# A two-layer vision tower on one core: the tokenizer's second chunk on 64 rows, layer 1's folded value weights earlier, the last image's rows ahead of its gate, and the last output rows on two queues

## The chip, the core and the metric

The kernel runs on one core of a Trainium2 chip. Five engines work side by side, each through its own instructions in order: PE (TensorE, matmuls and transposes; its weight loads are listed apart as PEld), DVE (VectorE), ACT (ScalarE), POOL (GpSimd) and SP (SyncE, which here only issues transfers). ACT, POOL and SP can each issue DMA transfers. The metric is the device time of one execution in microseconds (us). All data are 32-bit floats.

## What is computed

The input is four images of 3 x 224 x 224. Cut to what matters here, the reference does:

```python
patches = ...                               # [4, 784, 192], 8x8 pixels x 3 channels
t = layernorm(patches) @ W1 + b1            # 192 -> 256
t = layernorm(t)
t = concatenate([t, t, t], axis=1)          # 2352 tokens an image, three equal copies
h = silu(layernorm(t @ Wp1 + bp1)) @ Wp2 + bp2
# layer 0: softmax attention between the images (heads of 32), then an expert FFN
h = h + attn0(layernorm(h))                 # q, k, v, a sigmoid gate, output weights Wo
h = h + ffn0(layernorm(h))                  # router, top 2 of 6 experts, three matmuls each
# layer 1: linear attention, then a shared MLP and top 2 of 4 small experts
h = h + attn1(layernorm(h))                 # q, k, v from W_qkv; k^T v; (v + t2) @ W_out
h = h + ffn1(layernorm(h))
```

The three copies of a token are equal, so the kernel computes 4 x 784 tokens and writes each row three times.

## The kernel before

**Tiles.** An image's 784 tokens are six tiles of 128 and 16 rows left over. The leftover rows of all four images share a 25th tile, LT, in segments of 32 partitions. The rows h live in SBUF from the tokenizer to the end.

**Start.** The images arrive by DMA in `img` with 126 partitions (patch rows of the images, with gaps). `flatten` (L381) copies them into `vT`, group by group (7 groups of 4 patch columns), on DVE (groups 0, 3, 5) or ACT (1, 2, 4, 6); a patch takes 193 columns there: 192 pixels and, as the last, its standard deviation, which `patch_stats` (L487, DVE) and `patch_stds` (L494 to L497 on DVE, a square root L498 on ACT) make. `turn_patches` transposes a group on PE (L393) and copies it on ACT (L397) into `pT`: chunk 0 has 128 rows (pixels), chunk 1 has 65 (64 pixels and the deviation). `first_layers`, a generator that the stage advances with `next(steps)`, meanwhile folds the first layer norm into the weights `Wall`, 512 columns wide: 256 for the product and 256 that carry it on through Wp1.

**Tokenizer.** `first_steps` takes the tiles in seven groups `turns` of 4, 4, 4, 4, 3, 3 and 3. For each tile it runs two matmuls (L637), chunk 0 then chunk 1, then squares on ACT (L640); a square root (L642), DVE's `y` (L648 to L652), a second root (L655) and `xn` (L659) follow, then `turned_rows` (silu) and `last_rows`.

**Zero-fill.** The expert stage scatters rows into two DRAM buffers, `xrows` and `yrows`, which must be zero first. SP issues 46 transfers (L597) from an SBUF tile of zeros, `nothing`; each waits for `arrived[-1]`, the last patch statistics. Their SBUF bytes are later taken over by others: one of the buffers of `prod` (L907) lies on `nothing`.

**Layer 0's attention** begins while the tokenizer runs: `keys_values` makes keys (L320, pkv), values and gates of a group from its norm (L283 to L294, L701), adds the output bias to h (L1361), and `products` (L907, DVE) multiplies queries and keys of pairs of images. Then, image by image (s), come the shares of the softmax, `gate_act` (the gate's activation), `first_value`, `values`, `attended` (output weights, L989; sums of squares, L995), `rows_of_part` (the next norm's rows, L1025), `turn_part` (their transposes), the router, `choose`, `count` and `send` (POOL's scatters into xrows, L1154). For the last image the first expert blocks are woven in: `load` fetches a block's rows (L1498), `own_weights` (L1519) its weights, `hidden` (L1543, L1549) the hidden layers, `rows_back` (L1561, L1567) the last.

**Layer 1** takes units of three tiles and the leftover unit LU. `qk_mm` (L2001, PE), `qk_add` (L2007, DVE), `qk_squares` (L2015, L2016, ACT), `root` (L2033, ACT), `factors` (L2039 to L2043, DVE), `q_rows` (L2055, DVE) and `k_rows` (L2048, ACT) make normalised queries and keys; `stats_one` (L1767, L1784, L1785) sums a tile's expert outputs into h and takes its norm's statistics; `norm_root` is L1797 on ACT, and `norm_rows` L1806 and L1809 on DVE. `layer1_weights` is a generator of three steps: PE transposes the value weights (L812) and ACT copies them and a bias (L818, L819); PE multiplies them with the output weights (L825) and ACT copies the result Wvo (L829); the same for the bias (L834 to L837). Later, `k_x` (L2100), the norm of the keys (L2118 to L2126), Wvo and the output rows follow.

**FFN of layer 1** ends with the sums into h (L2410, L2415) and the output transfers (L2423). In the last group they alternate between SP's queue and ACT's; LT, the last tile, needs four transfers of 16 rows.

**What sets the order.** In these stages the order of each engine is that in which the program is written, by blocks `with tc.manual_schedule(engines=by_hand)` for DVE, PE and ACT (some for SP or POOL too). A moved call moves its instructions in every engine's queue at once.

Of the kernel before, what the change touches and what calls it, by code (L numbers as in the profile page):

```python
# [24 lines left out]
ALU = mybir.AluOpType  # L25
# [47 lines left out]
def tile_vit_tower(ctx: ExitStack, tc: tile.TileContext, a: dict, out: bass.AP):  # L73
# [296 lines left out]

    SROW = PD - P
    K1 = (P, SROW + 1)
    NPX = PD + 1
    flat = vT.rearrange("p c n -> p (c n)")[:IP, : HP * NPX].rearrange("q (w f) -> q w f", f=NPX)

    flattened = []

    def flatten(k, put):  # L380
        done = put(  # L381
            flat[:, k * PW : (k + 1) * PW, :PD].rearrange("q w (y x) -> q w y x", x=PATCH),
            img[:, :, k * PW * PATCH : (k + 1) * PW * PATCH].rearrange(
                "q y (w x) -> q w y x", x=PATCH
            ),
        )
        if put != nc.scalar.copy:
            flattened.append(done.ins.name)

    def turn_patches(k, c, put=nc.scalar.copy):  # L390
        pt, n = ps_tile("ptp"), K1[c]
        for j in range(PW):
            nc.tensor.transpose(  # L393
                pt[:n, j * IP : (j + 1) * IP], flat[:, k * PW + j, c * P : c * P + n],
                ident[:IP, :IP],
            )
        put(  # L397
            pT[:n, c, :, k * PW : (k + 1) * PW].rearrange("p (o h) w -> p o h w", o=SETS),
            pt[:n, : PW * IP].rearrange("p (w h o) -> p o h w", w=PW, h=HH)[:, :SETS],
        )  # L400

    def first_layers():

# [67 lines left out]
        for i in range(2):  # L471
# [2 lines left out]
            )  # L474
        nc.vector.memset(Wall[:, 0, D - 1 : D], 0.0)
        nc.vector.tensor_scalar(
            Wall[:, 1, D - 1 : D], ident[:, SROW : SROW + 1], math.sqrt(1e-5 * D), None, ALU.mult
        )
        yield
        nc.vector.tensor_tensor(bp1, pw, bp1, ALU.add)  # L480
# [9 lines left out]
    def patch_stds(k0, k1):  # L490
        w0, n = k0 * PW, (k1 - k0) * PW
        st, v = pst[:, w0 : w0 + n], pv[:, w0 : w0 + n]
        d = tokp.tile([IP, HP], F32, tag="pd", name="pd", bufs=2)[:, :n]
        nc.vector.tensor_tensor(d, st[:, :, 1], st[:, :, 4], ALU.subtract)  # L494
        nc.vector.tensor_tensor(v, st[:, :, 2], st[:, :, 5], ALU.add)
        nc.vector.scalar_tensor_tensor(d, d, PD / 4.0, d, ALU.mult, ALU.mult)
        nc.vector.tensor_tensor(v, v, d, ALU.add)  # L497
        nc.scalar.activation(  # L498
            flat[:, w0 : w0 + n, PD], v, AF.Sqrt, bias=eps[:IP], scale=1.0 / PD,
        )  # L500

    srow = tokp.tile([1, P], F32, tag="srow", name="srow")
# [5 lines left out]
    by_hand = {ENG.DVE, ENG.PE, ENG.Activation}  # L508
    with tc.manual_schedule(engines=by_hand):
        nc.vector.memset(srow, 0.0)  # L510
        nc.vector.memset(srow[:, SROW : SROW + 1], 1.0)
        nc.vector.memset(perm, 0.0)
        nc.vector.memset(perm[:, :, :PD], -1.0 / PD)
        by_y = ident[:KP, :KP].rearrange("p (y x c) -> p c y x", x=PATCH, c=CH)
        for half in range(2):
            nc.vector.tensor_scalar(
                perm[:, half, :PD].rearrange("p (c y x) -> p c y x", c=CH, x=PATCH)[
                    :, :, 4 * half : 4 * (half + 1)
                ],
                by_y, -1.0 / PD, None, ALU.add,  # L520
            )
        nc.scalar.activation(root_, one_, AF.Sqrt, bias=one_)
# [10 lines left out]
        flatten(0, nc.vector.tensor_copy)  # L533
        flatten(1, nc.scalar.copy)
        turn_patches(0, 0)
        for k in range(2):
            patch_stats(k)
        flatten(2, nc.scalar.copy)
        turn_patches(1, 0)
        for k in (3, 5):  # L540
            flatten(k, nc.vector.tensor_copy)
        next(steps)
        for k in range(2, cut0):
            patch_stats(k)
        turn_patches(2, 0)
        flatten(4, nc.scalar.copy)
        turn_patches(3, 0)
        flatten(6, nc.scalar.copy)
# [6 lines left out]
        for k in range(cut0):  # L555
            turn_patches(k, 1)
        for k in range(cut0, NK):
            patch_stats(k)
        next(steps)
        patch_stds(cut0, NK)  # L560
        for k in range(cut0, NK):
            turn_patches(k, 1)
# [51 lines left out]
    for c, n in enumerate(K1):  # L614
        nc.vector.tensor_copy(pL[:n, c, :, :LEFT], left(pTf[:n, c, :]))

    def pixels(c, t):
        if t == LT:
            return pL[: K1[c], c].rearrange("p b n -> p (b n)")
        n0 = t // TPI * SEQ + t % TPI * TT  # L620
        return pTf[: K1[c], c, n0 : n0 + TT]

# [4 lines left out]
    def first_steps(g):  # L627

        tiles = turns[g]
        n = len(tiles)  # L630
        y = tokp.tile([TT, GT, D], F32, tag="y", name="y", bufs=2)
        r = small.tile([TT, GT], F32, tag="rstd", name="rstd")[:, :n]
        pms = []
        for j in range(n):
            pm = ps_tile("pw1")[:TT]
            for c in range(2):
                nc.tensor.matmul(  # L637
                    pm, pixels(c, tiles[j]), Wall[: K1[c], c, :], start=(c == 0), stop=(c == 1)
                )
            nc.scalar.activation(sq1, pm[:, :D], AF.Square, accum_out=r[:, j : j + 1])  # L640
            pms.append(pm)
        nc.scalar.activation(r, r, AF.Sqrt, scale=1.0 / D, bias=zero[:TT])  # L642
        yield
        nc.vector.reciprocal(r, r)
        st = small.tile([TT, GT, 6], F32, tag="st", name="st")
        mv = small.tile([TT, GT, 2], F32, tag="mv", name="mv")
        for j in range(n):
            nc.vector.scalar_tensor_tensor(  # L648
                y[:, j, :], pms[j][:, D:], r[:, j : j + 1], bp1, ALU.mult, ALU.add
            )  # L650
            nc.vector.bn_stats(st[:, j, :], y[:, j, :])
# [929 lines left out]
    with tc.manual_schedule(engines=by_hand | {ENG.SP}):  # L1581
        gate_mm(s, 0)
        gate_mm(s, 1)
        products(s, 1, [1])
        expert_weights([2])
        scales_of(u)
        steps = early_blocks()
        next(steps)
        products(s, 1, [2])
        shifts_of(u)  # L1590
        next(steps)
        gate_act(s, 0)
        products(s, 1, [3])
        expert_weights(range(3, E0))
        next(steps)
        mx = shares_before(s)
        next(steps)
        gate_act(s, 1)
        shares_after(s, mx)
    att.close()  # L1600
    work[0] = layer0.enter_context(tc.tile_pool(name="blocks", bufs=2, reuse_waits="tile"))
# [4 lines left out]
    )  # L1606
    with tc.manual_schedule(engines=by_hand | {ENG.SP}):
        first_value(s, 0, 0, GN, nc.vector)
        first_value(s, 1, 0, GN, nc.scalar)
        rows_of_part(u)  # L1610
        values(s, 0, 0, GN)
        for _ in steps:
            pass
        for i in range(4):
            load(i)
        values(s, 1, 0, GN)
        turn_part(u)
        for o in range(2):
            first_value(s, o, *rest, nc.scalar)
        router(u)  # L1620
# [590 lines left out]
    with tc.manual_schedule(engines=by_hand | {ENG.Pool}):  # L2211
        x_t(1)
        for j in range(UT):
            qk_mm(0, j)
            qk_add(0, j)
            qk_squares(0, j)
        root(0)
        for j in range(UT):
            qk_mm(1, j)
        qk_add(1, 0)  # L2220
        qk_squares(1, 0)
        stats_one(LU, 0)
# [12 lines left out]
        root(1)  # L2235
        q_rows(0)
        stats_one(2, 0)
        next(steps)
        x_t(LU)
        q_t(0)  # L2240
        k_rows(0)
        next(steps)
        stats_one(2, 1)
        factors(1)
        q_rows(1)
# [113 lines left out]
    with tc.tile_pool(name="ffn1", bufs=2) as work:  # L2359
# [3 lines left out]
        for g, tiles in enumerate(parts):  # L2363
# [50 lines left out]
            for j, t in enumerate(tiles):  # L2414
# [4 lines left out]
                cuts = [(b, i * TT, 0, TT)]  # L2419
                if t == LT:  # L2420
                    cuts = [(k, TPI * TT, k * SEG, LEFT) for k in range(NI)]
                for k, s0, p0, rows_ in cuts:
                    eng.dma_start(  # L2423
                        out=out[k].rearrange("(k s) d -> s k d", k=REP)[s0 : s0 + rows_],
                        in_=h[p0 : p0 + rows_, t, :].unsqueeze(1).to_broadcast([rows_, REP, D]),
# [34 lines left out]
```

## Time and profile before

| what | us |
|---|---|
| median of 11 runs | 716.35 (715.01 to 719.26) |
| the profiled execution | 716.19 |
| its span | 714.5 |
| PE busy (matmuls) | 684.7, 96% of the span |
| PE weight loads | 474.5, 66% |
| DVE busy | 459.0, 64% |
| ACT busy | 331.4, 46% |
| POOL busy | 129.0, 18% |
| granted clock of PE, mean | 0.994 |

The profile comes from one execution, and its span runs from the first instruction to the end of the last; 1.69 us of the execution's time lie outside it. A row of a timeline has the start and the duration in us, the engine, the line of the program, the operation, what it writes and reads, its shape, how many instructions are joined in it, and in brackets the idle time ahead of it and what ended that. A group by line has, behind the bar, the busy time of the whole group in us, the mean of one in ns, and the idle time before. A row of the chain has start, duration and what was running, or what was waited for ("SPq" and "DVEq" are an engine's queue between a release and the start).

### The profile page before, as it was taken

The page shows a single profiled execution, that of the slowest core. Times are in us where ns is not written, and L with a number is a line of the kernel's source. Part 1 is how long each engine was busy: PE and PEld are TensorE (multiplying, and loading weights), DVE is VectorE, ACT ScalarE, POOL GpSimd, SP SyncE. Part 2 cuts the span into 40 slices and gives each one's busy share as a digit, 9 for nine tenths or more (in the row PEclk, how much of TensorE's full clock was granted, in tenths as well). Part 3 has the DMA queues.
Part 4 walks back from the last instruction along what each step waited for, and adds up shares of the span by engine and source line. Part 5 has one row for each costly group of instructions (what it writes and reads, how often), then busy time and mean ns, then how long its engine had stood idle before and what let it go on. Part 6 is the DMA issues. An engine that isn't in the chain of part 4 may idle for free.

```text
span 714.5 us, 9849 instructions
## 1 busy us (share of the span) xinstructions
PE 684.7 (96%) x3043; PEld 474.5 (66%) x3043; DVE 459.0 (64%) x1385; ACT 331.4 (46%) x816; POOL 129.0 (18%) x242
## 2 busy tenths in 40 slices
PE   7899999999999899999999998999999999999996
PEld 4646665566656678788888865667767844555553
DVE  5567785769888754457655658789869555344442
ACT  1556666556896664323222328464446132222321
POOL 5400000000045537300003218454000000000000
PEclk9999999999999899999999999999999999999999
DMA  5999999000034745322334342222000013332333
GB/s 185 286 426 424 425 424 424 27 1 0 0 100 158 265 156 180 122 83 97 96 106 143 102 132 81 68 66 67 0 1 1 4 31 122 121 100 72 112 99 91
DMA packets 56476, 96.49 MB, mean 135 GB/s; under 512 B 6696, under 2 KB 46350, under 8 KB 56424
## 3 DMA queue, kind: packets, MB, share of 16 engines
q1 hardware_dynamic: 49924, 79.69, 31.3%
q0 software_dynamic: 5600, 14.32, 6.6%
q10 hardware_dynamic: 900, 1.86, 0.8%
q8 instruction: 24, 0.39, 0.2%
q14 instruction: 28, 0.23, 0.1%
HBM read 30.75 MB, written 65.09 MB: 134 GB/s over the span
## 4 chain that ended last, share of the span: by engine, by line
PE 63%; DMA 16%; DVE 13%; ACT 4%; issue 2%; SPq 1%; ACTq 0%; DVEq 0%
DMA yrows<-nothing 14%; PE pb L1543 13%; PE pe L320 6%; PE pyb L1561 6%; PE ps L320 5%; PE pqk L2001 4%; PE ps L2410 3%; PE pt L311 3%; PE pout L2180 3%; PE pout L2185 3%; DVE oT L960 3%; PE pukx L2100 2%; PE pkv L320 2%; DMA img<-in_x_dram 2%; PE pe L2380 2%; PE ps L2404 2%
## 5 line engine op out<-in xcount | busy, mean ns | idle before, releaser
L1154 POOL DMA_INDIRECT xrows<-xn,pos x50 | 55.0, 1101 | 207.4 <-DVE nm L1010 172.6
L1753 POOL DMA_INDIRECT ys<-yrows,pos x50 | 49.5, 991 | 129.6 <-DMA yrows<-yb 115.3
L1549 ACT ACTIVATE hb<-pb,own 128x256 f32<-128x256 f32 (+1 forms) x74 | 33.6, 456 | 50.4 <-PE pb L1543 38.5
L1543 PE MATMUL pb<-xTb,own 128*128 128x256 f32 (+1 forms) x240 | 52.7, 362 | 2.0 <-DVE own L1519 1.3
L1543 PE MATMUL pb<-hb,own 128*128 128x256 f32 (+1 forms) x240 | 53.0, 360 | 0.3 <-DVE hb L1551 0.2
L1561 PE MATMUL pyb<-own,hb 128*128 128x256 f32 x216 | 52.3, 381 | 0.3 <-ACT hb L1549 0.2
L1543 PEld LDWEIGHTS pb<-xTb,own 128*128 128x128 f32 x240 | 41.9, 190 | 7.4 <-ACT junk L995 1.7
L320 PE MATMUL pe<-xT,eW 128*128 128x512 f32 (+1 forms) x112 | 46.0, 553 | 0.0
L2001 PE MATMUL pqk<-Wqkv,lxT 128*128 128x512 f32 x100 | 44.9, 594 | 0.2 <-ACT lxT L94 0.2
L1561 PEld LDWEIGHTS pyb<-own,hb 128*128 128x128 f32 x216 | 40.1, 190 | 6.3 <-ACT hb L1549 1.1
L1543 PEld LDWEIGHTS pb<-hb,own 128*128 128x128 f32 x240 | 40.7, 190 | 4.7 <-DVE hb L1551 0.9
L1567 DVE TENSOR_TENSOR yb<-pyb,eb 128x512 f32<-128x512 f32 (+1 forms) x30 | 19.1, 637 | 37.1 <-PE pyb L1561 35.3
L637 PE MATMUL pw<-Wall,pT 128*128 128x512 f32 (+1 forms) x96 | 42.4, 592 | 0.0
L1532 ACT COPY xTb<-ptb 128x512 f32<-128x512 f32 (+1 forms) x30 | 16.2, 541 | 53.6 <-PE ptb L1528 53.6
L907 DVE SCALAR_TENSOR_TENSOR prod<-kq 128x784 f32<-128x784 f32 x32 | 30.6, 969 | 7.3 <-ACT kq L882 3.9
L320 PEld LDWEIGHTS pe<-xT,eW 128*128 128x128 f32 x112 | 20.2, 190 | 21.6 <-issue 16.5
L1519 DVE COPY own<-kq 128x1540 f32 x30 | 29.0, 969 | 6.7 <-ACT xTb L1532 3.2
L311 PEld LDWEIGHTS pt<-ident,xn 128*128 128x128 f32 x200 | 24.3, 145 | 12.6 <-issue 6.9
L1551 DVE TENSOR_SCALAR hb<-pb,own 128x256 f32<-128x256 f32 (+1 forms) x46 | 20.3, 444 | 17.9 <-PE pb L1543 17.3
L637 PEld LDWEIGHTS pw<-Wall,pT 128*128 128x128 f32 (+1 forms) x96 | 17.9, 189 | 20.5 <-issue 18.5
L2001 PEld LDWEIGHTS pqk<-Wqkv,lxT 128*128 128x128 f32 x100 | 18.4, 190 | 19.3 <-issue 17.0
L2015 ACT ACTIVATE qk<-qk 128x256 f32<-128x256 f32 x50 | 20.4, 408 | 22.9 <-DVE qk L2007 20.8
(420 smaller groups left out, 1447.7 us busy)
## 6 DMA issues: line engine op xcount, KB each, us to landing
xrows<-nothing SPq DMA_DIRECT2D x22, 896.0 KB
yrows<-nothing SPq DMA_DIRECT2D x22, 896.0 KB
out_dram<-h SPq DMA_DIRECT2D x23, 384.0 KB
xb<-xrows SPq DMA_DIRECT2D x24, 256.0 KB
yrows<-yb SPq DMA_DIRECT2D x24, 256.0 KB
kq<-in_L_ffn_expert_w_dram SPq DMA_DIRECT2D x18, 256.0 KB
wb<-wd SPq DMA_DIRECT2D x16, 128.0 KB
img<-in_x_dram SPq DMA_DIRECT2D x5, 294.0 KB
```

Of the source, the lines that this page charges most:

```text
L311: nc.tensor.transpose(pt[:, j * TT : (j + 1) * TT], xn[:, j, c * P : (c + 1) * P], ident[:TT, :TT])
L320: nc.tensor.matmul(pm[: wcols.stop - wcols.start, :n], w[:, c, wcols], xT(c), start=(c == 0), stop=(c == chunks - 1),)
L637: nc.tensor.matmul(pm, pixels(c, tiles[j]), Wall[: K1[c], c, :], start=(c == 0), stop=(c == 1))
L907: nc.vector.scalar_tensor_tensor(prod, qTs[s][:, o, :], 1.0, kT[:, o, t * SEQ : (t + 1) * SEQ], ALU.mult, ALU.mult, accum_out=atts[s][:, o ...
L960: nc.vector.scalar_tensor_tensor(acc, vT[:, o, t * SEQ + n0 : t * SEQ + n0 + n], atts[s][:, o, t : t + 1], acc, ALU.mult, ALU.add,)
L1154: put = nc.gpsimd.indirect_dma_start(out=xrows[:, :], out_offset=bass.IndirectOffsetOnAxis(ap=pos[:, k, t0 + j : t0 + j + 1], axis=0), in_ ...
L1519: nc.vector.tensor_copy(w, ewf[0][:, bass.ds(off, EW)])
L1543: nc.tensor.matmul(pm, wm[:, c, o * P : (o + 1) * P], src[:, c, :], start=(c == 0), stop=(c == 1),)
L1549: nc.scalar.activation(dst[:, o, :], pm, AF.Relu, bias=b)
L1561: nc.tensor.matmul(pm[:, t, :], src[:, c, t * P : (t + 1) * P], wm[:, c, :], start=(c == 0), stop=(c == 1),)
L1753: got = nc.gpsimd.indirect_dma_start(out=y[:, j, k, :], out_offset=None, in_=yrows[:, :], in_offset=bass.IndirectOffsetOnAxis(ap=pos[:, k, ...
L2001: nc.tensor.matmul(pqk, xTs[u][:, c, cut(j, 1)], Wqkv[:, c, : 2 * D], start=(c == 0), stop=(c == 1),)
```

## The change

**Tokenizer.** A patch now takes 192 columns of `vT`. `flatten` subtracts the patch's pixels from its last one, so that the last column is zero and the deviation is put there instead; layer norm doesn't see a constant that is added to all pixels, and the folded weights change sign for it (`perm`). DVE does this for groups 0, 1, 2, 3 and 5 as one subtraction each, ACT for groups 4 and 6 as four activations each. Chunk 1 is exactly 64 rows. It is written into `pT` twice, on rows 0 to 63 by ACT and on rows 64 to 127 by DVE, and the weights `Wall` have their second chunk on both halves. `first_steps` runs the first chunks of a group's tiles, then their second chunks, alternately on the lower and on the upper 64 rows, then all squares. The transposes of chunk 1 (28 of them) move out of the start into group 0, between its first chunks and its second chunks.

```diff
+        for w in range(PW):
+            nc.scalar.activation(
+                to[:, w], src[:, w], AF.Identity, scale=-1.0, bias=ref[:, w : w + 1]
+            )
...
-        put(
-            pT[:n, c, :, k * PW : (k + 1) * PW].rearrange("p (o h) w -> p o h w", o=SETS),
-            pt[:n, : PW * IP].rearrange("p (w h o) -> p o h w", w=PW, h=HH)[:, :SETS],
-        )
+        for r, how in enumerate((put, nc.vector.tensor_copy)[: c + 1]):
+            how(
+                pT[r * n : (r + 1) * n, c, :, k * PW : (k + 1) * PW].rearrange(
+                    "p (o h) w -> p o h w", o=SETS
+                ),
+                pt[:n, : PW * IP].rearrange("p (w h o) -> p o h w", w=PW, h=HH)[:, :SETS],
+            )
...
+    def last_patches():
+        for k in range(NK):
+            turn_patches(k, 1)
+        nc.vector.tensor_copy(pL[:, 1, :, :LEFT], left(pTf[:, 1, :]))
...
-            for c in range(2):
-                nc.tensor.matmul(
-                    pm, pixels(c, tiles[j]), Wall[: K1[c], c, :], start=(c == 0), stop=(c == 1)
-                )
+            nc.tensor.matmul(
+                pm, pixels(0, tiles[j], slice(0, P)), Wall[:, 0, :], start=True, stop=False
+            )
+            pms.append(pm)
+        if g == 0:
+            last_patches()
+        for j, pm in enumerate(pms):
+            side = j % 2
+            ks = slice(side * HK, (side + 1) * HK)
+            nc.tensor.matmul(
+                pm, pixels(1, tiles[j], ks), Wall[ks, 1, :], start=False, stop=True
+            )
+        for j, pm in enumerate(pms):
             nc.scalar.activation(sq1, pm[:, :D], AF.Square, accum_out=r[:, j : j + 1])
-            pms.append(pm)
```

In the start's order, the second `next(steps)` of the folding now stands ahead of `flatten(6)`, and the one that was between the last statistics and the last deviations is gone from there.

**Last image.** The rows of the image before it (u) and its gate:

```diff
         next(steps)
+        rows_of_part(u, part=(0, 1))
         mx = shares_before(s)
         next(steps)
-        gate_act(s, 1)
         shares_after(s, mx)
...
         first_value(s, 0, 0, GN, nc.vector)
+        rows_of_part(u, part=(1, 4))
         first_value(s, 1, 0, GN, nc.scalar)
-        rows_of_part(u)
+        rows_of_part(u, part=(4, TPI))
...
+        turn_part(u)
+        gate_act(s, 1)
         values(s, 1, 0, GN)
-        turn_part(u)
```

**Layer 1.** The first two steps of `layer1_weights`:

```diff
             qk_squares(0, j)
+        next(steps)
         root(0)
         for j in range(UT):
             qk_mm(1, j)
+        next(steps)
         qk_add(1, 0)
         qk_squares(1, 0)
...
         stats_one(2, 0)
-        next(steps)
         x_t(LU)
         q_t(0)
         k_rows(0)
-        next(steps)
         stats_one(2, 1)
```

**Last rows.** All but the first of the last tile's output transfers go to ACT's queue. The added halving of the last tile applies only if that tile isn't LT; it is LT here, so nothing is halved.

```diff
+                elif t == parts[-1][-1]:
+                    cuts = [(b, i * TT + p, p, TT // 2) for p in (0, TT // 2)]
                 for k, s0, p0, rows_ in cuts:
+                    if t == parts[-1][-1] and p0:
+                        eng = nc.scalar
```

More of the change, by code (lines that the diff above doesn't have):

```diff
@@ L358, in cut, with flatten @@
         return slice(t0 * TT, (t0 + n) * TT)
-    SROW = PD - P
-    K1 = (P, SROW + 1)
-    NPX = PD + 1
+    HK = PD - P
+    NPX = PD
     flat = vT.rearrange("p c n -> p (c n)")[:IP, : HP * NPX].rearrange("q (w f) -> q w f", f=NPX)
     flattened = []
[L380 to L385, printed above, removed]
-        )
-        if put != nc.scalar.copy:
-            flattened.append(done.ins.name)
+    def flatten(k, eng):
+        to = flat[:, k * PW : (k + 1) * PW, :].rearrange("q w (y x) -> q w y x", x=PATCH)
+        src = img[:, :, k * PW * PATCH : (k + 1) * PW * PATCH].rearrange(
+            "q y (w x) -> q w y x", x=PATCH
+        )
+        ref = src[:, :, CH * PATCH - 1, PATCH - 1]
+        if eng is nc.vector:
+            done = nc.vector.tensor_tensor(
+                to, ref.unsqueeze(2).unsqueeze(3).to_broadcast([IP, PW, CH * PATCH, PATCH]),
+                src, ALU.subtract,
+            )
+            flattened.append(done.ins.name)
+            return
+        for w in range(PW):
+            nc.scalar.activation(
+                to[:, w], src[:, w], AF.Identity, scale=-1.0, bias=ref[:, w : w + 1]
+            )
     def turn_patches(k, c, put=nc.scalar.copy):
-        pt, n = ps_tile("ptp"), K1[c]
+        pt, n = ps_tile("ptp"), (P, HK)[c]
         for j in range(PW):
@@ L476, in first_layers @@
         nc.vector.tensor_scalar(
-            Wall[:, 1, D - 1 : D], ident[:, SROW : SROW + 1], math.sqrt(1e-5 * D), None, ALU.mult
+            Wall[:, 1, D - 1 : D], ident[:, HK - 1 : HK], ident[:, P - 1 : P],
+            math.sqrt(1e-5 * D), ALU.add, ALU.mult,
         )
@@ L498, in patch_stds @@
         nc.scalar.activation(
-            flat[:, w0 : w0 + n, PD], v, AF.Sqrt, bias=eps[:IP], scale=1.0 / PD,
+            flat[:, w0 : w0 + n, PD - 1], v, AF.Sqrt, bias=eps[:IP], scale=1.0 / PD,
         )
@@ L510, in tile_vit_tower @@
         nc.vector.memset(srow, 0.0)
-        nc.vector.memset(srow[:, SROW : SROW + 1], 1.0)
-        nc.vector.memset(perm, 0.0)
-        nc.vector.memset(perm[:, :, :PD], -1.0 / PD)
+        nc.vector.memset(srow[:, HK - 1 : HK], 1.0)
+        nc.vector.memset(srow[:, P - 1 : P], 1.0)
+        nc.vector.memset(perm[:, :, :PD], 1.0 / PD)
         by_y = ident[:KP, :KP].rearrange("p (y x c) -> p c y x", x=PATCH, c=CH)
@@ L519, in tile_vit_tower @@
                 ],
-                by_y, -1.0 / PD, None, ALU.add,
+                by_y, -1.0, 1.0 / PD, ALU.mult, ALU.add,
             )
+        nc.vector.memset(perm[:, :, PD - 1 : PD], 0.0)
+        nc.vector.tensor_copy(perm[:, :, PD:], perm[:, :, P:PD])
         nc.scalar.activation(root_, one_, AF.Sqrt, bias=one_)
@@ L532, in tile_vit_tower @@
             nc.tensor.transpose(warm[:, :P], ident, ident)
-        flatten(0, nc.vector.tensor_copy)
-        flatten(1, nc.scalar.copy)
+        flatten(0, nc.vector)
+        flatten(1, nc.vector)
         turn_patches(0, 0)
@@ L537, in tile_vit_tower @@
             patch_stats(k)
-        flatten(2, nc.scalar.copy)
+        flatten(2, nc.vector)
         turn_patches(1, 0)
         for k in (3, 5):
-            flatten(k, nc.vector.tensor_copy)
+            flatten(k, nc.vector)
         next(steps)
@@ L545, in tile_vit_tower @@
         turn_patches(2, 0)
-        flatten(4, nc.scalar.copy)
+        flatten(4, nc.scalar)
         turn_patches(3, 0)
-        flatten(6, nc.scalar.copy)
+        next(steps)
+        flatten(6, nc.scalar)
         for k in range(4, NK):
@@ L554, in tile_vit_tower @@
         patch_stds(0, cut0)
-        for k in range(cut0):
-            turn_patches(k, 1)
         for k in range(cut0, NK):
             patch_stats(k)
-        next(steps)
         patch_stds(cut0, NK)
-        for k in range(cut0, NK):
-            turn_patches(k, 1)
         next(steps)
@@ L613, in tile_vit_tower, with pixels @@
     pTf = pT.rearrange("p c q w -> p c (q w)")
-    for c, n in enumerate(K1):
-        nc.vector.tensor_copy(pL[:n, c, :, :LEFT], left(pTf[:n, c, :]))
-    def pixels(c, t):
+    nc.vector.tensor_copy(pL[:, 0, :, :LEFT], left(pTf[:, 0, :]))
+    def last_patches():
+        for k in range(NK):
+            turn_patches(k, 1)
+        nc.vector.tensor_copy(pL[:, 1, :, :LEFT], left(pTf[:, 1, :]))
+    def pixels(c, t, ks):
         if t == LT:
-            return pL[: K1[c], c].rearrange("p b n -> p (b n)")
+            return pL[ks, c].rearrange("p b n -> p (b n)")
         n0 = t // TPI * SEQ + t % TPI * TT
-        return pTf[: K1[c], c, n0 : n0 + TT]
+        return pTf[ks, c, n0 : n0 + TT]
     sq1 = tokw.tile([TT, D], F32, tag="sq1", name="sq1", bufs=1)
@@ L635, in first_steps @@
             pm = ps_tile("pw1")[:TT]
-            for c in range(2):
-                nc.tensor.matmul(
-                    pm, pixels(c, tiles[j]), Wall[: K1[c], c, :], start=(c == 0), stop=(c == 1)
-                )
+            nc.tensor.matmul(
[9 more added lines that the diff above has]
+                pm, pixels(1, tiles[j], ks), Wall[ks, 1, :], start=False, stop=True
+            )
+        for j, pm in enumerate(pms):
             nc.scalar.activation(sq1, pm[:, :D], AF.Square, accum_out=r[:, j : j + 1])
-            pms.append(pm)
         nc.scalar.activation(r, r, AF.Sqrt, scale=1.0 / D, bias=zero[:TT])
@@ L2219, in tile_vit_tower @@
             qk_mm(1, j)
+        next(steps)
         qk_add(1, 0)
@@ L2241, in tile_vit_tower @@
         k_rows(0)
-        next(steps)
         stats_one(2, 1)
```

## The prediction

> **What bounds the kernel now.** All sums go against the profiled execution: 716.19 us, of which 714.5 are span and 1.69 lie around it. The median of the runs is 716.35, so a sum against 716.19 may stand beside it as it is. About 0.2% (1.4 us) is what a measurement of this kernel can tell from no change: "the same" runs from 714.9 to 717.8.
>
> I read the engines' busy time first. PE is busy in 96% of the span, so PE time saved looks like time won. The chain that ended last contradicts this in one stretch: it gives 14% to a transfer, the zero-fill of the expert buffers. The next view is that chain around the end of the transfer:
>
> ```profile
> 24.34 2.10 DVE pst L487 x8
> 26.44 0.02 SPq L597
> ...
> 112.99 15.83 DMA yrows<-nothing
> 128.82 0.04 DVEq L907
> ```
>
> The zero-fill (L597) starts when the last patch statistics (L487) end, and its last piece lands at 128.82, where the product L907 on DVE gets its release. The timeline of DVE shows how much room was left:
>
> ```profile
> 129.38 0.95 DVE L1361 TENSOR_TENSOR h<-h,bo 128x768 f32<-128x768 f32 x1
> 130.25 0.97 DVE L907 SCALAR_TENSOR_TENSOR prod<-kq 128x784 f32<-128x784 f32 x1
> ```
>
> DVE reached this L907 at 130.25, so the transfer had 1.43 us to spare. In the changed kernel's instruction order this L907 still waits for all eight hardware DMA queues. Up to 130 us the kernel is a race of PE and DVE against the zero-fill, and PE's lead is worth 1.43 us at the most.
>
> In layer 1 the same chain passes through DVE from 430.84 to 443.47 almost without a break. There the timelines of ACT, DVE and PE carry the argument:
>
> ```profile
> 431.19 0.30 ACT L2033 ACTIVATE s<-s,zero 128x3 f32<-128x3 f32 x1
> 431.56 0.42 ACT L2015 ACTIVATE qk<-qk 128x256 f32<-128x256 f32 x1
> ...
> 433.15 0.29 ACT L1797 ACTIVATE rstd<-mv,eps 128x1 f32<-128x1 f32 x1 [0.28 <-DVE mv L1785]
> ```
> ```profile
> 434.24 0.15 DVE L1806 RECIPROCAL rstd<-rstd 128x1 f32<-128x1 f32 x1
> ```
> ```profile
> 438.11 2.00 PE L825 MATMUL pwvo<-Wout,WvT 128*128 128x256 f32 x8 [0.99 <-ACT WvT L819]
> ```
>
> ACT finishes a root, squares the next projection, makes rstd, and DVE takes it 0.8 us later. The weight products L825 come only after that, at 438.11.
>
> **Part 1, the tokenizer's second chunk on 64 rows, two tiles side by side.** The groups by line and shape say what a narrow chunk costs today:
>
> ```profile
> L637 PE MATMUL pw<-Wall,pT 65*128 65x512 f32 x48 | 24.6, 592 | 0.0
> L637 PE MATMUL pw<-Wall,pT 128*128 128x512 f32 x48 | 24.5, 592 | 0.0
> ```
>
> 65 rows cost what 128 cost. In the timeline 12 such passes take 5.35 us less the last one's overlap, a start each 0.43 us, and a tile's chunk is two passes, 0.86 us. No row of before shows two 64-row matmuls side by side. Nearest rows: in L2380 two column halves share the array, four 512-wide passes in 1.08 us where four full ones start over 1.72; in L2402 eight 256-wide passes on four row strips take 0.71 us against 1.99 for eight full ones (L2404). So strips on different rows do overlap. A pair then saves 0.7 to 0.86 us, and the seven groups (4, 4, 4, 4, 3, 3, 3 tiles) hold 11 pairs: 7.7 to 9.4 us of PE, or 0 if they don't overlap. I take 0.8 a pair, 8.8.
>
> Against it: all 28 second-chunk transposes and their copies move into group 0, between its first and second chunks. First chunks can start when the last first-chunk copy is done (about 28.5 instead of 30.47, since nothing of the second chunk precedes them) and take 3.5 us, to 32.0. Each of the seven copies is now two, and DVE's waits for ACT's: about 0.55 us each by the 65x448 rows (2.25 us for five), so the last ends at 36.5 to 36.9 and group 0's second chunk near 38 instead of 37.3. Its squares (0.57 us each) come after all of that, so group 0 loses about 1 us. Groups 0 to 2 then go at the pace of DVE's y and xn (4.3 us a group), and what reaches 130 us of the saving is 3.5 to 4.3 us.
>
> That cover is the zero-fill's, which now starts **later**. DVE flattens five groups by a subtraction instead of three by copies. A copy took 0.56 and 0.47 us; the nearest subtraction of that size is L1361 above, 0.95 alone and 0.87 in a row. From 16.99: 1.8 (two subtractions), 2.1 (eight statistics), 2.6 (three), 3.15 (twelve), 1.0 (the fix-ups of Wall, now ahead), 0.6 (deviations), 2.1 (eight): 30.4 against 26.44, 3.9 later. The transfer itself is 41.4 MB at the 424 GB/s of the page's slices, 97 us, and nothing shortens it; but its first microseconds shared the queues with leftover weights (some 0.6 MB, up to 2 us), which will now be through. So it ends 1.9 to 3.9 later; I take the middle, 2.7. L907 waits to about 131.5, which is 2.7 - 1.43 = **+1.3 us** (0.5 to 2.5). Behind it on DVE stands the norm whose 11.6 us chain ends at PE's key projection:
>
> ```profile
> 141.82 0.30 PEld L320 LDWEIGHTS pkv<-mT,Wk 128*128 128x128 f32 x2 [1.24 <-ACT mT L1317]
> ```
>
> So the whole delay reaches PE, and the PE time saved becomes idle time ahead of 131 and 143. **Part 1 gives nothing of its 8.8 us.**
>
> **Part 2, the value weights sooner (layer 1).** PE's side is a gain of 0.99 us at L825, but off the chain. The loss is on ACT. In the new order ACT has: squares of unit 0, bvs and WvT (0.48 + 0.57), root, then the two Wvo copies (L829), and only then squares(1,0) and rstd. The copies wait for L825, which PE reaches after all of unit 1's projections:
>
> ```profile
> 423.77 10.46 PE L2001 MATMUL pqk<-Wqkv,lxT 128*128 128x512 f32 x24
> 440.22 0.66 ACT L829 COPY Wvo<-pwvo 128x256 f32<-128x256 f32 x2
> ```
>
> The projections end at 434.2, 0.45 later with the four transposes ahead: 434.7. Eight passes of L825 at 0.216 bring 436.4, the copies 437.0. squares(1,0), at 431.56 before, begin there; three of 0.4 make 438.1, rstd 438.4. DVE's L1806 then runs at 438.45 instead of 434.24: **+4.2 us**. What is queued behind it on DVE (xaL, the third addition, q_rows, the expert sums) is the chain itself, and it hands on the whole delay, through rstd L1797 at 443.47 and the norm product at 450.39. ACT saves 1.7 us of copies there, but its next work waits for DVE. Bounds: 2.5, if DVE's next additions fill in and ACT catches up; 6 with PE's clock reduced.
>
> **Part 3, last image's rows before its gate.** Rows of u come earlier, ACT gets ahead by about 0.5 us, and PE's router and output passes by up to 1.2. Then the first expert block's weights wait as before, for the row transfer behind POOL's scatters:
>
> ```profile
> 251.10 0.96 DVE L1519 COPY own<-kq 128x1540 f32 x1 [0.45 <-DMA xb<-xrows]
> ```
>
> The gain is covered. In the new order an exponential falls between the two halves of the first block's hidden layer, so ACT's function table is loaded twice more (34 for 32). A load took 1.28 us in the timeline at 256.59, and one delays xT, for which PE's router (255.48) waits: **+1.1 us** (-0.8 if covered and the earlier rows count, +2 with both loads).
>
> **Part 4, last rows by two queues.** SP issues five output transfers from 708.47 in 3.58 us, 0.72 each, and the span ends with the last. Three of the leftover tile's four go to ACT, whose own issue took 0.40 us at 708.90. SP's last issue comes forward to 709.9, ACT's three from 709.31 end near 711.4 instead of 712.05: **-0.65 us** (0 to -1).
>
> The sum: 1.3 + 4.2 + 1.1 - 0.65 = +5.95, so 716.19 + 5.95 = **722.1 us**. The bounds of the parts give about 718 to 726.
>
> [...] The windows of before show what stalls do to PE's clock, columns being PE, PEld, DVE, ACT, POOL busy, granted clock, DMA share and GB/s:
>
> ```profile
> 231.00:234.00 3.00, 0.83 (x10) 0.57 (x9) 2.38 (x11) 2.24 (x6) 2.19 (x3) 1.00 0.51 168
> 234.00:237.00 3.00, 2.00 (x6) 1.12 (x7) 2.86 (x5) 3.00 (x7) 2.29 (x3) 0.56 1.03 358
> 237.00:240.00 3.00, 3.00 (x10) 2.08 (x9) 2.89 (x6) 2.85 (x7) 2.39 (x3) 0.50 1.06 361
> ```
>
> After 3 us with PE mostly idle the grant is about half for some 6.5 us, so that 3.25 us are lost if PE is the bound. The change makes three such stalls: two near 131 and 143, one from 436.5 to 440. I leave the dips out of the sum because the stalls are 2 to 4 us long, at the row's edge.
>
> [...]
>
> **Rivals.**
> - *The clock falls in the stalls.* For it: the windows above. Against: shorter stalls, and around 131 PE has transposes to do. One or two dips: 725 to 728. Chance 0.15.
> - *The Wvo copies delay nobody.* If PE takes L825 early or ACT's squares slip past without moving L1806, only 1.3 + 1.1 - 0.65 is left: 717.9. Against: each engine runs in the order shown. Chance 0.12.
> - *The other side: the zero-fill doesn't hold L907.* If the transfer ends ahead of DVE by more than PE gains (landing before about 126), the saving counts. Then -8.8 + 1 + 4.2 + 1.1 - 0.65 = -3.2: 713.0, faster. It needs an end 2.8 us earlier from a start that is later, at a queue already at 424 GB/s. Chance 0.07.
> - *The pairs don't overlap.* PE then gains nothing in part 1 and arrives at 130 about 1 us late, still ahead of 131.5. The time is the forecast's; only the spacing of matmuls tells. It is inside the forecast.
>
> **How the numbers follow.** The forecast has 0.62, the rivals 0.15, 0.12 and 0.07, other stalls 0.04. 718 to 726 leaves out the faster case (0.07), half of the second rival and the upper end of the first, about 0.18. Faster: 0.07. Same (up to 717.8): under half of the second rival and part of the rest, 0.09. Slower: 0.84.
>
> **What would show it.** Part 1: second-chunk matmuls in pairs, two passes a pair 0.43 us apart; last L487 near 30.4; the second L907 released by the zero-fill near 131.5, with PE idle before it. Part 2: squares(1,0) near 437 behind Wvo, L1806 waiting about 4 us for rstd. Part 3: `own` again released by xb, a table load inside the first block. Part 4: three leftover issues on ACT, the span's tail 0.65 us shorter. The forecast is wrong if the zero-fill starts near 26 still, if L1806 is not late, or if PE's saving is seen after 143.

## The result, and the profile after

The changed kernel takes 723.26 us (median of 9 runs, 722.82 to 726.08) against 716.56 for before (34 runs, 715.01 to 719.26): a ratio of 1.010, 95% interval 1.0089 to 1.0111, so 6.4 to 8.0 us slower. The forecast was 722.1, in 718 to 726. The profiled execution of the changed kernel took 726.44 us, with a span of 724.7: it lies 3 us above the median, above all the other runs, and has to be read with that in mind.

The page of the changed kernel shows at once that PE is busy only 0.9 us longer than before, in a span that is 10 us longer:

```profile
PE 685.6 (95%) x3043; PEld 471.1 (65%) x3043; DVE 465.0 (64%) x1396; ACT 334.9 (46%) x822; POOL 128.3 (18%) x242
```

To see where the time came from, I matched each instruction of the two traces with its twin and looked at how much later it starts. The difference (for PE) is a staircase:

| time in before, us | PE starts later by, us |
|---|---|
| 45 | +1.35 |
| 92 to 132 | -2.11 |
| 145 to 225 | +1.97 |
| 250 | +1.72 |
| 262 | +6.53 |
| 300 to 425 | +6.4 |
| 450 to 706 | +10.08 |
| end of the span | +10.26 |

So there are three steps, where the prediction put them: near 131, near 255 and near 435. Ahead of the first, PE wins 3.46 us between 45 and 92 us, by the paired passes. Between 231 and 250 us it runs up to 2.4 us ahead, with the rows that come earlier, and has lost that again at the first expert block. Elsewhere between the steps nothing changes by more than 0.2 us.

**The first step.** The timeline of DVE in the changed kernel (old lines L1361 and L907 are now L1382 and L928; the bracket holds the idle time ahead of an instruction):

```profile
127.28 0.95 DVE L1382 TENSOR_TENSOR h<-h,bo 128x768 f32<-128x768 f32 x1
131.82 0.97 DVE L928 SCALAR_TENSOR_TENSOR prod<-kq 128x784 f32<-128x784 f32 x1 [3.59 <-issue]
```

DVE is there 2.1 us sooner than before and then stands for 3.59 us. The row names no releaser ("issue"). The profile's answer on the zero-fill's line (L606 now) does, under those who waited for it:

```profile
  DVE prod L928: 3.6, 1
```

In the trace's semaphore records the zero-fill's last piece lands at 131.54, 2.72 us later than before, and L928 is held until 131.57. The product runs 1.57 us later than before. PE's timeline shows the key projection behind it, and the windows the clock (columns: PE, PEld, DVE, ACT, POOL busy, granted clock, DMA share, GB/s):

```profile
136.28 4.54 PE L320 MATMUL pkv<-mT,Wk 128*128 128x384 f32 x8 [3.00 <-ACT mT L1338]
```
```profile
134.00:137.20 3.20, 0.92 (x3) 0.65 (x4) 2.23 (x11) 2.12 (x6) 0.00 (x0) 1.00 0.00 0
137.20:140.60 3.40, 3.40 (x6) 1.60 (x6) 3.37 (x9) 0.82 (x2) 0.00 (x0) 0.50 0.00 0
```

PE waits 3.00 us, where it waited 0.62 before, and the next 3.4 us run at half clock. PE goes from 2.11 us ahead to 1.97 behind here, 4.08 us in all; DVE, 1.57 us late ahead of the half clock, is 1.97 late behind it, so the half clock's own share of the step is 0.4 us. That the zero-fill starts later stands in SP's queue:

```profile
29.70 0.36 SPq L606 DMA_DIRECT2D xrows<-nothing  x1
```

That is 3.2 us later than before (26.50), and the last piece lands 101.8 us after this start, where before it took 102.3 us.

**The second step.** ACT in the changed kernel, around the first expert block, and PE's router passes (L320) behind it:

```profile
255.88 0.45 ACT L1570 ACTIVATE hb<-pb,own 128x256 f32<-128x256 f32 x1
256.34 1.28 ACT L1305 ACT_TABLE_LOAD   x1
257.64 0.23 ACT L1305 ACTIVATE lg<-lg 128x36 f32<-128x36 f32 x1
257.78 0.46 ACT L1570 ACTIVATE hb<-pb,own 128x256 f32<-128x256 f32 x1
258.13 1.06 ACT L1060 COPY xT<-pt 128x512 f32<-128x512 f32 x2
```
```profile
258.76 2.53 PE L320 MATMUL pr<-xT,rw 128*128 128x512 f32 x4 [2.03 <-ACT xT L1060]
```
```profile
256.00:260.06 4.06, 2.03 (x10) 1.17 (x9) 1.28 (x7) 4.01 (x7) 0.00 (x0) 1.00 0.60 229
260.06:266.89 6.83, 6.83 (x20) 5.18 (x19) 1.38 (x6) 3.47 (x8) 1.97 (x2) 0.50 0.06 22
```

The table load stands between the two halves of the hidden layer, xT is late, PE idles for 2.03 us, and then the clock is halved for 6.83 us.

**The third step.** ACT and DVE in the changed kernel (rstd was L1797 and L1806, is L1820 and L1829):

```profile
442.00 0.37 ACT L850 COPY Wvo<-pwvo 128x256 f32<-128x256 f32 x1 [3.36 <-PE pwvo L846]
...
444.34 0.28 ACT L1820 ACTIVATE rstd<-mv,eps 128x1 f32<-128x1 f32 x1
```
```profile
444.65 0.16 DVE L1829 RECIPROCAL rstd<-rstd 128x1 f32<-128x1 f32 x1 [3.46 <-ACT rstd L1820]
```

ACT stands 3.36 us at the first copy of Wvo, and DVE 3.46 us at rstd, exactly in the chain that the prediction named.

**The end.** The last output transfers, by queue:

```profile
718.55 1.21 SPq L2450 DMA_DIRECT2D out_dram<-h  x2
718.99 3.36 ACTq L2450 DMA_DIRECT2D out_dram<-h  x4
```

ACT is now the last one, and ends at 722.35; moved back by the 10.08 us that all arrive late, that is 712.27 against SP's 712.05 before.

### The profile page after: what moved, and what is told of

Read it like the earlier page. It is cut to its first block, busy times and chain, and to the rows that moved or that the text cites. A ratio compares the mean times of both kernels' runs of the same rounds, so it can differ in the third digit from the quotient of the medians.

```text
span 724.7 us, 9872 instructions
## 1 busy us (share of the span) xinstructions
PE 685.6 (95%) x3043; PEld 471.1 (65%) x3043; DVE 465.0 (64%) x1396; ACT 334.9 (46%) x822; POOL 128.3 (18%) x242
## 4 chain that ended last, share of the span: by engine, by line
PE 57%; DVE 4%; ACT 3%; issue 1%; DMA 1%; DVEq 0%; ACTq 0%; SPq 0%
PE pb L1564 13%; PE pe L320 6%; PE pyb L1582 6%; PE pqk L2024 5%; PE ps L320 5%; PE ps L2433 3%; PE pout L2203 3%; PE pout L2208 3%; PE pukx L2123 2%; PE pt L311 2%; PE pe L2403 2%; PE ps L2427 2%; PE ptb L1549 1%; PE pkvo L2183 1%; DVE h L1790 1%
## 5 line engine op out<-in xcount | busy, mean ns | idle before, releaser
L1564 PE MATMUL pb<-hb,own 128*128 128x256 f32 (+1 forms) x240 | 54.8, 369 | 0.2
L2024 PE MATMUL pqk<-Wqkv,lxT 128*128 128x512 f32 x100 | 46.9, 613 | 0.2 <-ACT lxT L94 0.2
L320 PE MATMUL pe<-xT,eW 128*128 128x512 f32 (+1 forms) x112 | 46.0, 553 | 0.0
L928 DVE SCALAR_TENSOR_TENSOR prod<-kq 128x784 f32<-128x784 f32 x32 | 30.6, 969 | 11.1 <-ACT kq L903 3.9
L320 PEld LDWEIGHTS pe<-xT,eW 128*128 128x128 f32 x112 | 20.2, 190 | 21.6 <-issue 16.5
L311 PE MATMUL pt<-ident,xn 128*128 128x128 f32 x200 | 29.9, 286 | 1.7 <-DVE xn L680 1.2
L2024 PEld LDWEIGHTS pqk<-Wqkv,lxT 128*128 128x128 f32 x100 | 18.7, 195 | 19.6 <-issue 17.1
L101 ACT ACTIVATE e<-pe,cols 128x512 f32<-128x512 f32 (+1 forms) x26 | 16.8, 647 | 25.8 <-PE pe L320 25.8
```

Source lines behind the costliest of these rows:

```text
L311: nc.tensor.transpose(pt[:, j * TT : (j + 1) * TT], xn[:, j, c * P : (c + 1) * P], ident[:TT, :TT])
L320: nc.tensor.matmul(pm[: wcols.stop - wcols.start, :n], w[:, c, wcols], xT(c), start=(c == 0), stop=(c == chunks - 1),)
L928: nc.vector.scalar_tensor_tensor(prod, qTs[s][:, o, :], 1.0, kT[:, o, t * SEQ : (t + 1) * SEQ], ALU.mult, ALU.mult, accum_out=atts[s][:, o ...
L1564: nc.tensor.matmul(pm, wm[:, c, o * P : (o + 1) * P], src[:, c, :], start=(c == 0), stop=(c == 1),)
L2024: nc.tensor.matmul(pqk, xTs[u][:, c, cut(j, 1)], Wqkv[:, c, : 2 * D], start=(c == 0), stop=(c == 1),)
```

## The experiments

All ratios are against the kernel before, run beside each kernel in the same set. In the three sets (the parts alone; the two of the zero-fill's release, the first b_half and c_late; the rest) before took 717.49, 736.97 and 733.43 us. In the second and third set all profiled kernels lose, against the profile of before, 7 to 10 us between 265 and 300 and 4 to 8 us near 485, where rows go to DRAM and come back; why is not settled here. Their ratios have wide intervals, but up to 210 us their traces run like the first set's, except for a stretch of half clock near 26 us in two of them.

**Theory**: three queue waits make the loss (L907 behind the zero-fill, rstd behind the Wvo copies, xT behind a table load), and the halved clock comes on top where PE idles for them. **Rivals**: the row pairs don't overlap; the halved clock is most of it; the moved steps cost by themselves.

**1. Each part alone.** The edits are the four parts of the diff, each put into the kernel before by itself.

> The kernel before with the tokenizer's part alone. Theory (zero-fill): the second product L907 waits for the zero-fill, which starts 3.2 us later, and PE's saving is idle time; +1.6 us at the product (131.8 against 130.25), +1.5 to +2.0 us in all, and PE some 2 us ahead of before at 130 us. Rival (pairs): the two tiles don't overlap, and what is lost is PE time in the tokenizer; then PE is level with before or behind it at 130 us. Rival (clock): the loss is a half-clock stretch after PE's idle time near 135; then +0 us without such a stretch and +2 with one.

Measured: 1.0018 (1.0004 to 1.0032), +1.3 us. In its trace PE is 2.15 us ahead from 100 to 130 us, and 1.91 behind from 150 us. So the pairs do overlap, and the lead is lost at one place. As for the clock: the trace has a stretch of half clock at 136.95, but DVE is 1.50 us late ahead of it and 1.91 behind it, so that it adds 0.4 us. And of its runs the three with a mean granted clock of 0.996 or 0.997 took 717.5 to 718.5 us, where before's at 0.994 to 0.997 took 716.0 to 716.3: the loss is there at an equal clock too.

> The kernel before with layer 1's weight steps moved, alone. Theory (ACT's queue): the two Wvo copies wait for PE ahead of the squares and of rstd, and DVE's L1806 waits for that: +3.6 to +4.2 us, all of it between 431 and 445 us. Rival (absorbed): other work fills the wait, -0.5 to +0.5. Rival (clock): most of it is half clock of PE; then no more than about +1.7 without a half-clock stretch near 440.

Measured: 1.0036 (1.0022 to 1.0049), +2.6 us, less than the theory. The waits are the same to the hundredth as in the changed kernel:

```profile
435.43 0.37 ACT L829 COPY Wvo<-pwvo 128x256 f32<-128x256 f32 x1 [3.36 <-PE pwvo L825]
```
```profile
438.09 0.16 DVE L1806 RECIPROCAL rstd<-rstd 128x1 f32<-128x1 f32 x1 [3.46 <-ACT rstd L1797]
```

and what stands behind 450 us is 3.5 us later than in before, 3.7 us more than just ahead of 425, a 3.41 us stretch of half clock at 441 included. DVE is 3.9 us late at rstd already, at 438.09, and the half clock begins only at 441.44: it is not the cause. The experiment with the output queues, below, tells what before loses there too.

> The kernel before with the last image's rows ahead of its gate, alone. Theory (table loads): two more loads of ACT's function table, of which one delays xT by 1.3 to 2 us: +1 to +2 us. Rival (clock): PE's idle time there sets off a stretch of half clock of 6.8 us, as in the profile of the changed kernel (260 to 267 us): +4.4 us. Rival (gain): the rows come earlier and the first block follows: -0.5 us.

Measured: 1.0043 (1.0028 to 1.0058), +3.1 us: between the two figures. Its trace has PE's wait of 2.03 us and the clock behind it, this time for half as long:

```profile
258.49 3.67 PE L320 MATMUL pr<-xT,rw 128*128 128x512 f32 x4 [2.03 <-ACT xT L1039]
```
```profile
258.50:261.90 3.40, 3.40 (x4) 1.49 (x5) 0.75 (x3) 3.37 (x6) 0.00 (x0) 0.50 0.03 11
```

The four passes take 3.67 us instead of 1.98. The times of this kernel spread widely, 716.89 to 722.27. The lowest is its one run with a mean granted clock of 0.996, 0.8 us above before's at such a clock; those at 0.990 have a median of 720.8, against 718.6 for before's at 0.990. So both the wait and the clock behind it are in the 3.1 us.

> The kernel before with three of the last tile's four output transfers on ACT's queue, alone. The prediction had -0.65 us. After the profile of the changed kernel (four issues on ACT take 3.36 us where five on SP took 3.58) the theory is +0.2 us: ACT's issues of 16 rows take about 1 us each, so ACT is the last one now. Rival: SP is relieved and the end comes 0.65 us sooner.

Measured: 1.000 (0.9989 to 1.0012), no difference. Its profile has the four issues on ACT at 3.37 us, as in the changed kernel. Its value is elsewhere: layer 1 is as in before, and yet the windows differ. First the kernel before, then this one:

```profile
439.20:442.60 3.40, 3.40 (x14) 2.19 (x13) 3.12 (x11) 2.99 (x8) 2.93 (x5) 1.00 0.00 0
```
```profile
439.20:442.60 3.40, 3.40 (x8) 2.31 (x7) 3.11 (x11) 2.77 (x8) 3.19 (x4) 0.51 0.00 0
```

The same instructions ran at half clock in this execution, and what follows is 1.1 us later. The traces of the parts "a" and "c" alone, which have layer 1 as in before too, show the same stretch at 441 and 443. Of the ten traces in which layer 1 is as in before, five have it. So it is a matter of the execution, and the profile of before that the prediction was made from is one without it. Before's runs show the same: the 33 of this set have a median of 717.49; ten with a mean granted clock of 0.990 have one of 718.6, and only three have the profile's 0.994 or more, with one of 716.1.

The sum of the four parts is 1.3 + 2.6 + 3.1 + 0 = 7.0 us, and all together measured 6.4 to 8.0: the parts add up. How much of it is the clock in the median can be estimated from these runs: the changed kernel's lie at 0.986 to 0.991, 0.988 in the middle, before's in this set at 0.992 in the middle, and before's are 2.5 us faster at 0.994 than at 0.990. That makes some 2.5 us of the 6.7: a part, and not most of it.

**2. The zero-fill.** Part "a" with the transfer released earlier:

```diff
-                put.ins, arrived[-1],
+                put.ins, arrived[0],
```

> The tokenizer's part alone, with the zero-fill released by the first patch statistics instead of the last, so that it starts right behind the weights on SP's queue (about 25.6 us instead of 29.7). Theory (zero-fill): L907 no longer waits beyond 128.5, PE keeps its lead of 2.1 us past 145 us, and no half-clock stretch follows at 137: -1.5 to -2.2 us against before, 3 to 4 us under the tokenizer's part alone. Rival (pairs): the part's loss doesn't come from the zero-fill, and the time stays within 0.7 us of the part alone (+1.4).

Measured: 0.9998 (0.9979 to 1.0016). The transfer starts at 25.32, 4.4 us sooner than in the changed kernel, and its last piece lands at 129.25, 2.3 us sooner and still after DVE's arrival. It is issued right behind weights that are still under way: its first packets come 2.3 us after the issue, in the changed kernel 0.9. The product (L928) of this kernel:

```profile
129.54 0.98 DVE L928 SCALAR_TENSOR_TENSOR prod<-kq 128x784 f32<-128x784 f32 x1 [1.50 <-issue]
```

PE's lead is 2.31 us ahead of it and 0.72 behind it: 1.6 us of it are lost here instead of 4.1, and no half clock follows. The theory's mechanism holds, its amount (1.5 to 2.2 us of gain) doesn't, because the wait was only shortened.

> The kernel before, with the zero-fill released by the first patch statistics instead of the last. Control: the theory says that before's DVE comes to L907 at 130.25, 1.4 us behind the transfer's end, so an earlier end gives nothing: 0, within 0.7 us. If the zero-fill costs before more than L907 (shared queues, a port), it shows here.

Measured: 1.0004 (0.9989 to 1.0019). In its trace nothing moves between 30 and 225 us (+0.61 to +0.66 throughout), although the transfer starts 2.7 us sooner: before doesn't wait for it.

A stricter test takes the wait away: four small tiles are made ahead of the tile of zeros, so that it lies further up and the buffer of `prod` no longer on it. The transfer stays late.

```diff
+    srow = tokp.tile([1, P], F32, tag="srow", name="srow")
+    pst = tokp.tile([IP, HP, 6], F32, tag="pst", name="pst")
+    pv = tokp.tile([IP, HP], F32, tag="pv", name="pv")
+    bp1 = tokp.tile([TT, D], F32, tag="bp1", name="bp1")
     nothing = tokp.tile([P, 7 * D], F32, tag="nothing", name="nothing")
```

> The tokenizer's part alone, with the tile of zeros placed 3.2 KB further up in SBUF (four small tiles are made ahead of it), so that the buffer of the product L907 no longer lies on it and no longer waits for the zero-fill; the transfer itself is as late as in the changed kernel. Theory (zero-fill): L907 runs at about 128.1, PE keeps its lead of 2.1 us, and no half clock follows at 137: -1.8 to -2.3 us against before. Rival (shared resources): the late transfer costs by its mere overlap, and the time stays at the part's +1.4.

Measured: 0.9981 (0.9955 to 1.0007), 731.31 against 733.43. The zero-fill starts at 30.07, later than in any other kernel, its last piece lands at 132.78, and the product follows its predecessor at once:

```profile
128.68 0.95 DVE L1382 TENSOR_TENSOR h<-h,bo 128x768 f32<-128x768 f32 x1
129.55 0.97 DVE L928 SCALAR_TENSOR_TENSOR prod<-kq 128x784 f32<-128x784 f32 x1
```

PE is 0.71 us ahead at 100 us and 0.70 at 210 us: nothing is lost at the product any more. So the wait for the zero-fill, not its overlap, is the cause of the first step. That the lead is 0.7 here and not 2.1 is a half-clock stretch at 25.6 us, in the start. The other kernel with the moved tile (experiment 5) has it too, at 26.2, and the three with the tokenizer's part and the tile in its old place don't; whether it belongs to the moved tile or to the execution is open.

```profile
25.60:29.10 3.50, 3.46 (x15) 2.98 (x16) 3.36 (x18) 2.62 (x7) 2.25 (x5) 0.51 0.91 261
```

The interval of the time holds the theory's gain (0.997) as well as no gain, but not the part's own 1.0018.

**3. Layer 1's first step only.**

```diff
             qk_squares(0, j)
+        next(steps)
         root(0)
...
         stats_one(2, 0)
-        next(steps)
         x_t(LU)
```

> The kernel before with only the first of layer 1's weight steps (transposes, bvs, WvT) moved ahead of the root; the second (L825 and the two Wvo copies) stays where it was. Theory (ACT's queue): the cost sat in the Wvo copies, so it is gone: -0.7 to +0.3 us against before, with L825 no longer waiting 0.99 us for WvT. Rival: bvs and WvT, 1.05 us of ACT ahead of the root, cost about 1 us by themselves.

> Only the first weight step moved, once more on another chip. Theory (the Wvo copies hold the cost): within 0.7 us of before, where both steps moved gave +2.6. Rival (bvs and WvT ahead of the root cost by themselves): +0.8 to +1.2.

Measured in two sets: 1.0017 (0.9994 to 1.004) and 0.9986 (0.9958 to 1.0014). DVE doesn't wait at rstd in the first one's trace:

```profile
446.65 0.16 DVE L1806 RECIPROCAL rstd<-rstd 128x1 f32<-128x1 f32 x1
```

So the 3.46 us belong to the Wvo copies, as the theory has it. Whether bvs and WvT, 1.05 us of ACT ahead of the root, cost something themselves stays open: up to the same place the traces give +1.2 us and +0.5 us, of which 0.44 comes from the four transposes that now stand ahead of PE's projections, and in the first of them 0.5 from a wait for a row transfer.

**4. The last image's part without the extra table loads.** The exponentials of that part's router weights are put by hand behind the first block's xTb:

```diff
         turned(1)
+        mix1(u)
         shifts_of(ub)
```

> The last image's part alone, with the two exponentials of the router's weights put by hand behind the first block's xTb, so that ACT loads its function table 32 times as before and not 34. Theory (table loads): xT of the next part is no longer late and PE's 2 us of idle time ahead of its router passes goes, and with it the half clock behind it: -0.5 to +0.7 us against before, some 3 us under the part alone. Rival: the rows' new place itself costs, and +2 to +3 us stay.

> The last image's part with the exponentials by hand once more, beside other kernels and on another chip. Theory (table loads): -0.5 to +0.7 us against before, where the part alone had +3.1. Rival: +2 to +3 us stay.

Measured: 0.9991 (0.9969 to 1.0013) and 1.0017 (0.999 to 1.0043). In the first one's trace the router passes no longer wait:

```profile
257.89 0.60 PE L1533 MATMUL ptb<-ident,xb 128*128 128x128 f32 x4
258.33 1.95 PE L320 MATMUL pr<-xT,rw 128*128 128x512 f32 x4
```

The wait is gone with the loads. But in these sets PE waits 2.5 to 3 us for the first block just ahead of this place, and that would hide a part of any cost; that the moved rows are free by themselves is likely and not shown.

**5. What is left of the gain.** Part "a" with the tile of zeros moved, and part "c" with its exponentials by hand:

> The tokenizer's part with the tile of zeros moved (as above), and the last image's part with its two exponentials placed by hand; the weight steps and the output queues as before. If both theories hold: -1.5 to -3 us against before, the fastest of these kernels. If the last image's part costs by itself: -0.5 to +1.

Measured: 0.9989 (0.9969 to 1.0008). It is not shown to be faster than before, and neither is part "a" with the tile moved; the intervals of both lie below the changed kernel's 1.0089 to 1.0111.

## Why the prediction was right, and where it was not

The total was right: +5.95 forecast, 6.4 to 8.0 measured, and its three places are those of the staircase. By terms:

- **Part 1, +1.3 forecast, +1.3 measured** (0.3 to 2.3). L907 was expected at 131.5 and came at 131.82. Two errors nearly cancel, so the close hit is partly luck: the start of the zero-fill was expected 3.9 us later and was 3.2; of the up to 2 us that shared queues were to give back, 1.2 were taken (the prediction's middle of 1.9 to 3.9 is 2.9, not the 2.7 it writes) and 0.5 came. PE's saving was put at 0.7 to 0.86 us a pair:

```profile
38.67 3.70 PE L649 MATMUL pw<-Wall,pT 128*128 128x512 f32 x8
42.30 1.99 PE L658 MATMUL pw<-Wall,pT 64*128 64x512 f32 x8
```

The two passes of a pair start 0.01 us apart, and the pair takes the time of one full pass, 0.43 us. Around the change from full to narrow passes some 0.1 us is lost at each of three places (see below), so that a group of four tiles takes 5.45 us (to PE's next instruction at 44.12) where sixteen full passes would start over 6.88: 0.72 a pair, 0.58 in the groups of three, some 7.5 us in all instead of 8.8. From 45 to 92 us PE wins 3.46 us, about the lower end of the 3.5 to 4.3 that were to reach 130 us; it had lost 1.35 before. All of this lead became idle time, in one wait of 3.00 us at 136.28, not in two near 131 and 143: the half clock behind it puts PE back by another 1.7 us, where the prediction had the second wait.
- **Part 2, +4.2 forecast, +2.6 measured** (1.6 to 3.5): the mechanism was right and the size too large. Against the profile of before, the step is 3.7 us, and its times are those forecast (the copies at 437.0, found 436.8; rstd at 438.4, found 438.2, both less the 6.43 us that all are late there). The term failed in what it was compared with: before has a stretch of half clock of its own at 440 in some executions, 1.1 us, which its profiled execution hadn't. The trace of one execution was taken for the median. By the run times and clocks above, the profiled execution, 716.19, lies 1.3 us under the median of before's runs in that set, and the part's profiled one 0.2 under its own: 3.7 - 1.3 + 0.2 = 2.6, the whole difference.
- **Part 3, +1.1 forecast, +3.1 measured** (2.0 to 4.2): the largest error. The table load and its victim (xT, then PE's router passes) were right. The term was taken too small: one load was charged for 1.1 us; it held PE for 2.03, and the clock that fell after it was left to a rival. "The gain is covered" was right: the up to 2.4 us by which PE is ahead near 240 are gone at the first block.
- **Part 4, -0.65 forecast, 0.0 measured** (-0.8 to +0.9): the step that failed took 0.7 us for each 16-row issue on ACT, as on SP. The 0.72 was a mean over unequal issues: on SP before, the leftover tile's four take 0.35, 0.42, 1.38 and 0.43 us; on ACT now its three take 0.68, 1.42 and 0.68. One of them is long on either queue, the others cost 0.25 to 0.3 more on ACT. The transfers saved on one queue came back on the other.
- **The clock.** The prediction left the dips out of the sum and gave them 0.15 as a rival. In the changed kernel's profile two of the three that it named did come (137 and 448), and one at 260 that it hadn't named. In that execution half clock makes 17.1 us (3.41 + 3.41 + 6.83 + 3.41) against before's 6.83, so up to 5.1 of its 10.2 us. The median is smaller than the sum with all the dips, because they don't come in every execution. The runs show it: the changed kernel's go from 722.8 us at a mean granted clock of 0.991 to 726.1 at 0.986. Three dips of 3.25 us on top of the sum, one for each stall, would have made 732, too high for the median and for the profiled execution. The sum without the dips was 1.2 us too low, and that it came so near is partly luck: part 2 was 1.6 us too high, parts 3 and 4 together 2.65 too low.
- **The rivals.** "The Wvo copies delay nobody" is refuted by DVE's 3.46 us. "The zero-fill doesn't hold L907" is refuted for this kernel, and the kernel with the tile moved shows what it would have been. "The pairs don't overlap" is refuted by the rows above. "The clock falls in the stalls", one or two dips, is what the profiled execution shows, and its 725 to 728 holds that execution's 726.44, not the median.

## What to carry to other kernels

Ahead of a saving on the busiest engine, look for the next thing that the stage waits for and how much room it leaves: 1.43 us of room here decided over 8.8 us of PE time. A copy out of PSUM that is moved forward is put into the queue of its engine, and stands there in front of everything else until its producer is done: here 3.36 us at the first copy of Wvo, and 3.46 us for DVE behind it. And one profile is one execution: where the clock can fall (from 439.2 to 442.6 us it was 1.00 in one execution and 0.51 in another), compare medians, and look at the granted clock of every run before a microsecond is put down to an edit.

## What the runs showed of the hardware

- In the profiles of before and of the changed kernel the stretches of half clock last 3.41 or 6.83 us (but for those that the span's end cuts). In the changed kernel they start at 137.18, 236.17, 260.06 and 447.80, which is 98.99, 23.89 and 187.73 us apart, or 29, 7 and 55 times the length of the first, 3.413 us. After the same idle time a stretch came in one execution and none in another: ahead of L825 PE waits 0.99 us in before's profile and 0.98 in that of the output queues alone, and from 439.2 to 442.6 the clock is 1.00 in the first and 0.51 in the second.
- A wait of 2.03 us, with PE busy for 2.03 of 4.06 us, was followed by 6.83 us of half clock at 260.06 in the changed kernel, and the same wait by half as much of it, 3.40 us from 258.50, in the last image's part alone. That wait is shorter than the 3 us, 0.83 of them busy, that stand ahead of the half clock in the prediction's windows (231 to 234).
- The change from passes on 128 rows to passes on 64 cost PE a little here: in the rows of part 1 above, passes or pairs start 0.43 us apart, but the first narrow pair starts 0.52 us after the last full pass, the second pair 0.53 after the first, and PE's next instruction on full rows 0.52 after the last pair (63.04, in the group behind). What takes the 0.1 us at each place is not shown.
- ACT's first instruction after the table load of the second step starts with the load's end: 256.34 + 1.28, and the exponential at 257.64. Behind 28 of the 34 loads in that profile it starts 0.01 us after the end.
